# Mixing and decay products as pairs in the two halves of the matmul array, with row differences taken whole from SBUF, in an RWKV block

## The chip, the core and the metric

The kernel runs on one NeuronCore of a Trainium2 chip. The metric is the device time of one execution in microseconds (us); lower is better. The core has five engines with a queue of instructions each: PE (TensorE, matrix products), DVE (VectorE), ACT (ScalarE), POOL (GpSimd) and SP (SyncE, which issues most transfers here). All data are float32. SBUF is the working memory with 128 partitions; products land in PSUM.

## The reference

One RWKV-6 block for 32 sequences of 128 steps and 512 channels, 32 heads of 16. Cut to what matters:

```
xn = layernorm(x, ln1); sx = previous row of xn - xn
xxx = tanh((xn + sx * maa_x) @ maa_w1)            # 5 x 32 columns
x5[m] = xn + sx * (maa_stack[m] + xxx[m] @ maa_w2[m])     # 32 rows of maa_w2 for each m
w = exp(-exp(time_decay + tanh(x5[1] @ decay_w1) @ decay_w2))     # 64 columns, 64 rows
r, k, v = x5[3] @ Wr.T, x5[0] @ Wk.T, x5[2] @ Wv.T;  g = silu(x5[4] @ Wg.T)
for each step:  a = k outer v;  out = r . (u * a + s);  s = a + w * s
x = x + (groupnorm(out) * g) @ Wo.T
xn2 = layernorm(x, ln2); sx2 = previous row of xn2 - xn2
xk = xn2 + sx2 * ffn_maa_k;  xr = xn2 + sx2 * ffn_maa_r
x = x + sigmoid(xr @ Wr'.T) * (square(relu(xk @ Wk'.T)) @ Wv'.T)
```

The `@ maa_w2[m]` (contraction over 32) and `@ decay_w2` (over 64) are the mixing and decay products of the title. The differences to the previous row are taken in both norms.

## The kernel before

The 32 sequences go in 8 groups (`g`) of 4; a group has 512 columns (4 sequences x 128 steps), and the 512 channels stand as 4 blocks (`e`, `f` or `c`) of 128 partitions. Each group passes through these streams, written as Python generators:

- `front_mix`: loads x, normalizes and transposes it (`layernorm_T`), forms the mix `xin`, multiplies by maa_w1 (L414, and L417 with 32 output columns for the fifth mix), tanh, then 20 mixing products (5 mixes x 4 blocks, L435). Each is followed on DVE by two operations that read PSUM (L440 `(p + maa) * sx`, L442 `+ xn`).
- `front_proj`: the decay (L461 with 64 output columns, tanh, 4 products over 64 rows at L469, two exponentials on ACT), then k, r and v with full weights (`matmuls`, L382); `front_gate`: the gate.
- `prep` and the recurrence `rec_*`: 256 units in all. In each, POOL forms k v (L665) and a sum of pairs (L669), ACT copies the decays (L640), DVE scans (L687) and multiplies by r (L689), and PE sums by transposes (L722).
- `back`: group norm, gate, Wo (L810), second norm (`layernorm_T` again), then xk, xr, and the three FFN products (L382, L884, L900). The last group's `back` runs as two halves.

No queue order is left to the hardware. A planner (`Plan`) keeps a list of streams, gives each step a cost and a due time (the table `DUE`), and always emits the step that could start earliest, those within `EPSILON` of it by due time. The order in which it emits is the order of each engine's queue. It also hands out the buffers: "ps" are four PSUM tiles of 128x512 that nearly all products share, "mx" three SBUF tiles, "xnT" and "sx" one each. Steps marked `port=True` are ones that it doesn't plan beside POOL's.

In the before version the small weights are stored so that a mixing product uses the whole array: `w2p` holds for each of four mixes its 32 rows in their own place among zeros, so the contraction runs over all 128 rows of `tha`; the fifth mix shares the tile `dw2m` with the decay.

The row differences and mixes are made block by block in `layernorm_T`'s callback `use`. Each transposed block stays in its PSUM tile. ACT first writes its scaled form to `xnT` (L358), then scales it in place in PSUM (L403, L830); DVE takes the difference or the mix from `xnT` and that PSUM tile (L406 and L408 in the first norm, L833 in the second). For xr ACT writes a scaled copy into a further PSUM tile (L843) and DVE adds (L845).

Of the kernel before, what the change touches and what calls it, by code (L numbers as in the profile page):

```python
# [14 lines left out]
P = 128  # L15
# [23 lines left out]
PE_GAP = 0.04  # L39

# [3 lines left out]
EPSILON = 0.02  # L44


DUE = {"rec": (0.073, 0.928), "mix": (-1.183, -0.487), "proj": (-1.108, 0.725), "gate": (-0.487, 0.788), "prep": (11.173, 11.194), "back": (1.114, 2.212), "last1": (-8.358, -8.236), "last2": (1.752, 11.136)}
# [23 lines left out]
class Plan:  # L71
# [64 lines left out]
    def run(self):  # L136
        while self.streams:
# [32 lines left out]
            for b in op.end:  # L170
                (b if isinstance(b, Buf) else new[b]).open = False
            self.advance(st, new)
# [7 lines left out]
def rwkv6_block(ctx: ExitStack, tc: tile.TileContext, x, prev, s0, vecs, u, maa_w1, maa_w2,  # L180
# [19 lines left out]
    def tag(pool, shape, name, bufs):  # L200
# [13 lines left out]
        (big, [P, N], "tha", 1), (big, [P, N], "th", 2),  # L214
# [9 lines left out]
    ffn = const.tile([P, 3, NE], F32, name="ffn")  # L224
    u_sb = const.tile([P, S], F32, name="u_sb")
    w1_sb = const.tile([P, NE, 5 * XM], F32, name="w1_sb")
    w2p = const.tile([P, 4, E], F32, name="w2p")
    dw1_sb = const.tile([P, NE, XD], F32, name="dw1_sb")

    dw2m = const.tile([P, E], F32, name="dw2m")  # L230
# [8 lines left out]

    nc.gpsimd.memset(thb.t, 0.0)  # L240
    nc.gpsimd.memset(dw2m, 0.0)
    nc.vector.memset(w2p, 0.0)

    def constants():
        nc.sync.dma_start(out=vec, in_=vecs)
        nc.gpsimd.tensor_scalar(ffn[:, 0, :], vec[:, V_FK, :], -1.0, 1.0, ALU.mult, ALU.add)
        nc.gpsimd.tensor_scalar(ffn[:, 2, :], vec[:, V_FR, :], -1.0, 1.0, ALU.mult, ALU.add)
        nc.gpsimd.tensor_tensor(ffn[:, 1, :], ffn[:, 0, :], vec[:, V_LN2B, :], ALU.mult)
        nc.gpsimd.tensor_tensor(ffn[:, 0, :], ffn[:, 0, :], vec[:, V_LN2W, :], ALU.mult)
        nc.sync.dma_start(out=pv, in_=prev)  # L250
        nc.sync.dma_start(out=w1_sb, in_=maa_w1.rearrange("(c p) o -> p c o", p=P))
        for m in range(4):
            nc.sync.dma_start(out=w2p[m * XM : (m + 1) * XM, m, :], in_=maa_w2[m * XM : (m + 1) * XM, :])
        nc.sync.dma_start(out=dw2m[XD : XD + XM, :], in_=maa_w2[4 * XM : 5 * XM, :])
        nc.sync.dma_start(out=dw1_sb, in_=decay_w1.rearrange("(c p) o -> p c o", p=P))
        nc.sync.dma_start(out=dw2m[0:XD, :], in_=decay_w2)
        for e in range(NE):
            nc.sync.dma_start(out=lanes(u_sb, e), in_=u[e * HE : (e + 1) * HE, :].unsqueeze(0).to_broadcast([GB, HE, S]))
# [51 lines left out]
    def layernorm_T(g, src, sums, vw, vb, which, use, take, need=None, bs=range(GB)):  # L310

# [44 lines left out]
        def evict(e, pt):  # L356
            yield Op(ACT, part(0.78, bs), r=[(pt, None)], w=[(xnT, e)])
            nc.scalar.activation(xnT[:, e * GB + b0 : e * GB + b0 + nb_, 1 : L + 1], bt(pt[:, cols]), AF.Identity,  # L358
                                 bias=col(vb, e), scale=col(vw, e))
            yield from use(xnT, e, pt, tiles)  # L360

        for e in range(NE):
            if e == 0:
                pt, *tiles = yield Op(PE, 0.11 * nb_, r=[(xh, None)], w=[(0, None)], alloc=["ps", *take])
            else:
                (pt,) = yield Op(PE, 0.11 * nb_, r=[(xh, None)], w=[(0, None)], alloc=["ps"])
# [7 lines left out]
        return (xnT, *tiles)  # L374

    def row(xnT, e, shift, bs=range(GB)):

        return xnT[:, e * GB + bs[0] : e * GB + bs[-1] + 1, shift : shift + L]

    def matmuls(p, w, xin, e, cols=slice(0, N)):  # L380
        for c in range(NE):
            nc.tensor.matmul(p, lhsT=w[:, c, e * P : (e + 1) * P], rhs=xin[:, c, cols], start=(c == 0), stop=(c == NE - 1))  # L382

# [10 lines left out]
    def front_mix(g, d):  # L394
# [5 lines left out]
        def use(xnT, e, pt, tiles):  # L400

            yield Op(ACT, 0.75, w=[(pt, None)])
            nc.scalar.activation(pt.t, pt.t, AF.Identity, bias=col(V_LN1B, e), scale=col(V_LN1W, e))  # L403
            sx, xin = tiles
            yield Op(DVE, 0.69, r=[(xnT, e), (xnT, "p"), (pt, None)], w=[(sx, e)])
            nc.vector.tensor_tensor(bt(sx[:, e, :]), row(xnT, e, 0), bt(pt.t), ALU.subtract)  # L406
            yield Op(DVE, 0.75, r=[(pt, None), (sx, e)], w=[(xin, e)], end=[pt])
            nc.vector.scalar_tensor_tensor(xin[:, e, :], sx[:, e, :], col(V_MAAX, e), pt.t, ALU.mult, ALU.add)  # L408

        xnT, sx, xin = yield from layernorm_T(g, xt, None, V_LN1W, V_LN1B, 0, use, ("sx", "mx"), need)  # L410
# [5 lines left out]
        for c in range(NE):  # L416
            nc.tensor.matmul(pm2[XD : XD + XM, :], lhsT=w1_sb[:, c, 4 * XM : 5 * XM], rhs=xin[:, c, :],  # L417
                             start=(c == 0), stop=(c == NE - 1))
        (tha,) = yield Op(ACT, 0.6, r=[(pm, None)], w=[(0, None)], alloc=["tha"], end=[pm])
        nc.scalar.activation(tha.t, pm.t, AF.Tanh)  # L420
        yield Op(ACT, 0.6, r=[(pm2, None)], w=[(thb, None)], end=[pm2],
                 need=(lambda: "mixed" in data[g - 1]) if g else None)
        nc.scalar.activation(thb[XD : XD + XM, :], pm2[XD : XD + XM, :], AF.Tanh)

        for m in (1, 0, 3, 2, 4) if g else (1, 0, 2, 3, 4):

            lo, w2 = (tha.t, w2p[:, m, :]) if m < 4 else (thb.t, dw2m)
            x5, late = None, []
            for e in range(NE + 1):
                if e < NE:  # L430
                    if x5 is None:
                        pp, x5 = yield Op(PE, 2 * PASS, r=[(thb, None)], w=[(0, None)], alloc=["ps", "mx"])
                    else:
                        (pp,) = yield Op(PE, 2 * PASS, r=[(thb, None)], w=[(0, None)], alloc=["ps"])
                    nc.tensor.matmul(pp.t, lhsT=w2[:, e * P : (e + 1) * P], rhs=lo, start=True, stop=True)  # L435
                    late.append(pp)
                if e > 0:
                    pp, f = late.pop(0), e - 1
                    yield Op(DVE, 0.75, r=[(sx, None)], w=[(pp, None)])
                    nc.vector.scalar_tensor_tensor(pp.t, pp.t, col(V_MAA + m, f), sx[:, f, :], ALU.add, ALU.mult)  # L440
                    yield Op(DVE, 0.69, r=[(pp, None), (xnT, None)], w=[(x5, f)], end=[pp])
                    nc.vector.tensor_tensor(bt(x5[:, f, :]), bt(pp.t), xnT[:, f * GB : (f + 1) * GB, 1 : L + 1], ALU.add)  # L442
            d["x5", m] = x5
# [3 lines left out]
    def front_proj(g, d):  # L447
# [12 lines left out]
        for c in range(NE):  # L460
            nc.tensor.matmul(pd[0:XD, :], lhsT=dw1_sb[:, c, :], rhs=x5[:, c, :], start=(c == 0), stop=(c == NE - 1))  # L461
        (dlo,) = yield Op(ACT, 0.6, r=[(pd, None)], w=[(0, None)], alloc=["blk"], end=[pd])
        nc.scalar.activation(dlo[0:XD, :], pd[0:XD, :], AF.Tanh)
        late = []
        for e in range(NE + 1):
            if e < NE:
                (p,) = yield Op(PE, 2 * PASS, r=[(dlo, None)], w=[(0, None)], alloc=["ps"],
                                end=[dlo] if e == NE - 1 else [])
                nc.tensor.matmul(p.t, lhsT=dw2m[0:XD, e * P : (e + 1) * P], rhs=dlo[0:XD, :], start=True, stop=True)  # L469
                late.append(p)  # L470
            if e > 0:
                p, f = late.pop(0), e - 1
# [272 lines left out]
    def back(g, d, bs=range(GB), W=None):  # L745
# [81 lines left out]
        def use(xnT, e, pt, tiles):  # L827

            yield Op(ACT, part(0.75, bs), w=[(pt, None)])
            nc.scalar.activation(pt[:, cols], pt[:, cols], AF.Identity, bias=ffn[:, 1, e : e + 1], scale=ffn[:, 0, e : e + 1])  # L830
            (xk,) = tiles
            yield Op(DVE, part(0.75, bs), r=[(xnT, e), (xnT, "p"), (pt, None)], w=[(xk, e)], end=[pt])
            nc.vector.scalar_tensor_tensor(bt(xk[:, e, cols]), row(xnT, e, 0, bs), col(V_FK, e), bt(pt[:, cols]),  # L833
                                           ALU.mult, ALU.add)

        def receptance(xnT):
            xr = None
            for e in range(NE):
                if xr is None:
                    pr, xr = yield Op(ACT, part(0.75, bs), r=[(xnT, e)], w=[(0, None)], alloc=["ps", "mx"])  # L840
                else:
                    (pr,) = yield Op(ACT, part(0.75, bs), r=[(xnT, e)], w=[(0, None)], alloc=["ps"])
                nc.scalar.activation(bt(pr[:, cols]), row(xnT, e, 1, bs), AF.Copy, scale=ffn[:, 2, e : e + 1])  # L843
                yield Op(DVE, part(0.75, bs), r=[(xnT, e), (pr, None)], w=[(xr, e)], end=[pr])
                nc.vector.scalar_tensor_tensor(bt(xr[:, e, cols]), row(xnT, e, 0, bs), col(V_FR, e), bt(pr[:, cols]),  # L845
                                               ALU.mult, ALU.add)
            return xr

# [112 lines left out]
```

## Time and profile before

| | before |
|---|---|
| time, median of 3 runs | 1585.48 us (1584.49 to 1586.62) |
| profiled execution, its own time | 1586.62 us |
| its span, first to last instruction | 1584.8 us |
| PE busy | 1470.4 us |
| DVE busy | 1321.9 us |
| POOL busy | 919.0 us |
| ACT busy | 632.7 us |
| mean granted TensorE clock | 0.974 |

Busy time is the union of an engine's instructions within the span. A float32 product of 128 rows, 128 columns and 512 moving columns appears as two weight loads (PEld) and two matmul instructions, each with its own row; successive ones start 0.429 us apart at full clock, while each lasts some 0.59 us, since they are pipelined. In groups, a row gives line, engine, operation, output<-inputs, shapes and count, then busy time and mean duration, then the idle time just before and what ended it. "The chain" is followed back from the last instruction, at each step to what released it.

### The profile page before, as it was taken

The page shows a single profiled execution, that of the slowest core. Times are in us where ns is not written, and L with a number is a line of the kernel's source. Part 1 is how long each engine was busy: PE and PEld are TensorE (multiplying, and loading weights), DVE is VectorE, ACT ScalarE, POOL GpSimd, SP SyncE. Part 2 cuts the span into 40 slices and gives each one's busy share as a digit, 9 for nine tenths or more (in the row PEclk, how much of TensorE's full clock was granted, in tenths as well). Part 3 has the DMA queues.
Part 4 walks back from the last instruction along what each step waited for, and adds up shares of the span by engine and source line. Part 5 has one row for each costly group of instructions (what it writes and reads, how often), then busy time and mean ns, then how long its engine had stood idle before and what let it go on. Part 6 is the DMA issues. An engine that isn't in the chain of part 4 may idle for free.

```text
span 1584.8 us, 16299 instructions
## 1 busy us (share of the span) xinstructions
PE 1470.4 (93%) x5216; PEld 771.2 (49%) x5216; DVE 1321.9 (83%) x1702; ACT 632.7 (40%) x1213; POOL 919.0 (58%) x549
## 2 busy tenths in 40 slices
PE   5898799899989999999999999999999999978778
PEld 2344354355544554455554555544544555455444
DVE  5539899999989999989979999888988999697642
ACT  4233243345334352444444343443534443336242
POOL 3027683678746694468654694466843884687400
PEclk9999899999999999999999999999999999988989
DMA  6120232514142231423324232332413233240130
GB/s 216 54 83 24 92 97 74 169 60 127 47 143 80 67 120 51 139 88 98 101 71 139 77 117 75 123 104 64 122 50 113 92 107 95 72 140 27 39 121 27
DMA packets 126790, 146.86 MB, mean 93 GB/s; under 512 B 8080, under 2 KB 76304, under 8 KB 125680
## 3 DMA queue, kind: packets, MB, share of 16 engines
q1 hardware_dynamic: 91888, 129.03, 25.0%
q10 hardware_dynamic: 34816, 16.79, 3.7%
q8 instruction: 41, 0.67, 0.2%
q14 instruction: 45, 0.37, 0.1%
HBM read 94.41 MB, written 17.83 MB: 71 GB/s over the span
## 4 chain that ended last, share of the span: by engine, by line
PE 68%; DVE 17%; POOL 8%; issue 3%; ACT 1%; DMA 1%; SPq 0%; DVEq 0%; POOLq 0%
PE ps L382 26%; PE acc L722 10%; PE ps L435 7%; PE ps L884 7%; PE ps L900 6%; PE ps L810 6%; POOL am L665 5%; DVE sc L687 3%; POOL a L669 3%; DVE rm L689 2%; DVE ps L440 2%; PE ps L469 2%; PE ps L461 1%; DVE mx L442 1%; PE ps L417 1%
## 5 line engine op out<-in xcount | busy, mean ns | idle before, releaser
L665 POOL TENSOR_TENSOR am<-v,k 128x1024 f32<-128x1024 f32 x256 | 615.5, 2404 | 211.9 <-DVE k L564 111.2
L382 PE MATMUL ps<-mx,wt 128*128 128x512 f32 (+1 forms) x1312 | 576.3, 587 | 13.4 <-DVE mx L845 5.1
L669 POOL TENSOR_TENSOR a<-am 128x504 f32<-128x504 f32 x256 | 274.9, 1074 | 305.7 <-DVE sc L687 279.0
L382 PEld LDWEIGHTS ps<-mx,wt 128*128 128x128 f32 x1312 | 244.3, 191 | 288.5 <-issue 265.7
L689 DVE TENSOR_TENSOR rm<-sc,r 128x1024 f32<-128x1024 f32 x256 | 312.5, 1221 | 43.1 <-PE acc L722 30.0
L687 DVE TENSOR_TENSOR_SCAN sc<-sc,a 128x512 f32<-128x512 f32 x256 | 312.9, 1222 | 15.9 <-POOL a L669 13.1
L722 PEld LDWEIGHTS acc<-by_head,rm 128*128 128x128 f32 x2176 | 251.6, 143 | 130.9 <-issue 75.1
L722 PE MATMUL acc<-by_head,rm 128*128 128x128 f32 x2176 | 281.4, 276 | 19.7 <-DVE rm L689 12.8
L640 ACT COPY sc<-w 128x512 f32<-128x512 f32 x256 | 151.0, 592 | 233.3 <-DVE rm L689 181.5
L435 PE MATMUL ps<-tha,w2p 128*128 128x512 f32 x256 | 137.2, 634 | 20.7 <-DVE mx L442 5.9
L440 DVE SCALAR_TENSOR_TENSOR ps<-ps,vec,sx 128x512 f32<-128x512 f32 x160 | 119.8, 749 | 39.3 <-PE ps L435 38.9
L651 ACT COPY a<-st 128x8 f32<-128x8 f32 x256 | 50.9, 203 | 189.4 <-DVE sc L687 173.7
L884 PE MATMUL ps<-wt,mx 128*128 128x512 f32 x256 | 115.4, 593 | 4.2 <-DVE mx L408 2.7
L810 PE MATMUL ps<-wt,mx 128*128 128x512 f32 x256 | 116.6, 604 | 1.4 <-DVE x L819 1.4
L442 DVE TENSOR_TENSOR mx<-ps,xnT 128x512 f32<-128x512 f32 x160 | 110.5, 690 | 5.1
L900 PE MATMUL ps<-wt,ev 128*128 128x512 f32 x224 | 100.8, 592 | 0.0
L501 ACT COPY blk<-ps 128x512 f32<-128x512 f32 x96 | 55.9, 583 | 63.1 <-PE ps L382 62.9
L810 PEld LDWEIGHTS ps<-wt,mx 128*128 128x128 f32 x256 | 47.8, 193 | 59.9 <-issue 53.0
L884 PEld LDWEIGHTS ps<-wt,mx 128*128 128x128 f32 x256 | 47.4, 190 | 60.4 <-issue 59.1
L435 PEld LDWEIGHTS ps<-tha,w2p 128*128 128x128 f32 x256 | 43.1, 198 | 61.4 <-issue 21.3
L343 POOL TENSOR_TENSOR rstd<-rstd,mhalf 128x4 f32<-128x4 f32 (+1 forms) x17 | 16.7, 981 | 93.0 <-DVE rstd L341 92.6
L889 DVE SCALAR_TENSOR_TENSOR ps<-th,ps 128x512 f32<-128x512 f32 x32 | 22.1, 689 | 50.6 <-PE ps L900 47.2
(105 smaller groups left out, 1318.0 us busy)
## 6 DMA issues: line engine op xcount, KB each, us to landing
x<-in_x SPq DMA_DIRECT2D x15, 1024.0 KB
wt<-in_wk SPq DMA_DIRECT2D x8, 1024.0 KB
wt<-in_wr SPq DMA_DIRECT2D x8, 1024.0 KB
wt<-in_wg SPq DMA_DIRECT2D x8, 1024.0 KB
dgate<-blk SPq DMA_DIRECT2D x32, 256.0 KB
wt<-in_wo SPq DMA_DIRECT2D x8, 1024.0 KB
wt<-in_fk SPq DMA_DIRECT2D x8, 1024.0 KB
wt<-in_fr SPq DMA_DIRECT2D x8, 1024.0 KB
```

The lines of the kernel that those rows point to most:

```text
L382: nc.tensor.matmul(p, lhsT=w[:, c, e * P : (e + 1) * P], rhs=xin[:, c, cols], start=(c == 0), stop=(c == NE - 1))
L435: nc.tensor.matmul(pp.t, lhsT=w2[:, e * P : (e + 1) * P], rhs=lo, start=True, stop=True)
L440: nc.vector.scalar_tensor_tensor(pp.t, pp.t, col(V_MAA + m, f), sx[:, f, :], ALU.add, ALU.mult)
L640: nc.scalar.copy(sc.t, d["w01"][:, q : q + 1, :].to_broadcast([P, DH, T2]))
L665: nc.gpsimd.tensor_tensor(am.t, v[:, ds, :], k[:, q : q + 1, :].to_broadcast([P, DH, L]), ALU.mult)
L669: nc.gpsimd.tensor_tensor(a[:, :, 1:T2], am2[:, :, 0 : T2 - 1, 0], am2[:, :, 0 : T2 - 1, 1], ALU.add)
L687: nc.vector.tensor_tensor_scan(scf, scf, a.t.rearrange("p d n -> p (d n)"), 0.0, ALU.mult, ALU.add)
L689: nc.vector.tensor_tensor(pair(rm.t), sc.t.unsqueeze(3).to_broadcast([P, DH, T2, 2]), r2[:, q : q + 1, :, :].to_broadcast([P, DH, T2, 2]), ...
L722: nc.tensor.matmul(acc[:, i, :], lhsT=rm[:, i, :], rhs=by_head, is_transpose=True, start=(q == 0 and i % 4 == 0), stop=(q == S), skip_grou ...
L810: nc.tensor.matmul(p.t, lhsT=att[:, c, b * L : (b + 1) * L], rhs=wot[:, c, :], start=(c == 0), stop=(c == NE - 1))
L884: nc.tensor.matmul(p.t, lhsT=xr[:, c, b * L : (b + 1) * L], rhs=frt[:, c, :], start=(c == 0), stop=(c == NE - 1))
L900: nc.tensor.matmul(p2.t, lhsT=kv[:, c, b * L : (b + 1) * L], rhs=fvt[:, c, :], start=(c == 0), stop=(c == NE - 1))
```

## The change

- A mixing product contracts over 64 rows (32 of weights, 32 of zeros), a decay product over its 64. Two products, of two neighbouring column blocks of the output, are issued one after the other (`side_by_side`): one in the upper half of the array's rows, one in the lower half, into two PSUM tiles. The small weights (`w2p`, `dw2p`) hold the even blocks in partitions 0 to 63 and the odd blocks in 64 to 127.
- The low-rank rows must stand in both halves: `tha` gets a second plane with its halves exchanged (two more tanh of 64 partitions each), the fifth mix's columns of maa_w1 stand twice in `w1_sb` (so that L417's product has 96 output columns), and decay_w1 stands twice (128 output columns).
- The two evictions of each product are streams of their own (`mixed`), due right after the pair; a pair waits in the plan until all but one of the earlier products are evicted.
- The constants come in 26 loads in place of 14.
- The row differences and mixes change too: ACT only writes `xnT`, DVE takes one difference over the whole tile (`sx`), and `mix` makes xin, xk and xr by one operation per block, with both inputs in SBUF. The in-place scalings on ACT, the callback `use`, `receptance` and the tile `ffn` go.
- The planner's price for a pair is `PAIR`; the due times and `EPSILON` have other values.

```
+PAIR = 2.6 * PASS
-EPSILON = 0.02
+EPSILON = 0.0284
-DUE = {"rec": (0.073, 0.928), "mix": (-1.183, -0.487), "proj": (-1.108, 0.725), "gate": (-0.487, 0.788), "prep": (11.173, 11.194), "back": (1.114, 2.212), "last1": (-8.358, -8.236), "last2": (1.752, 11.136)}
+DUE = {"rec": (-0.719, 0.83), "mix": (-2.052, -0.463), "proj": (-0.981, -0.21), "gate": (-0.039, 0.771), "prep": (-0.013, 0.421), "back": (1.215, 2.03), "last1": (-10.118, 2.886), "last2": (-4.571, -2.72)}
...
+        for i, m in ((0, 1), (1, 2), (2, 0), (3, 3), (4, 4), (6, 4)):
+            nc.sync.dma_start(out=w1_sb[:, :, i * XM : (i + 1) * XM], in_=w1v[:, :, m * XM : (m + 1) * XM])
+        for h in range(2):
+            for m in range(5):
+                r = h * XD + (XM if m in (2, 3) else 0)
+                nc.sync.dma_start(out=w2p[r : r + XM, m, :].rearrange("r (f p) -> r f p", p=P),
+                                  in_=halves(maa_w2[m * XM : (m + 1) * XM, :], h))
...
+        (sx,) = yield Op(DVE, part(2.3, bs), r=[(xnT, None)], w=[(0, None)], alloc=["sx"], port=True)
+            nc.vector.tensor_tensor(
+                sx.t.rearrange("p e (b t) -> p (e b) t", t=L), xnT[:, :, 0:L], xnT[:, :, 1 : L + 1], ALU.subtract)
...
+    def mix(xnT, sx, v, bs=range(GB)):
+        for e in range(NE):
...
+            nc.vector.scalar_tensor_tensor(bt(o[:, e, b0 * L : b1 * L]), bt(sx[:, e, b0 * L : b1 * L]), col(v, e),
+                                           xnT[:, e * GB + b0 : e * GB + b1, 1 : L + 1], ALU.mult, ALU.add)
...
+    def side_by_side(pp, w, up, low):
+        for p, h, t in zip(pp, (slice(0, XD), slice(XD, P)), (up, low)):
+            nc.tensor.matmul(p.t, lhsT=w[h, :], rhs=t[h, :], start=True, stop=True)
...
+        nc.scalar.activation(tha[:, 0, :], pm.t, AF.Tanh)
+        nc.scalar.activation(tha[0:XD, 1, :], pm[XD:P, :], AF.Tanh)
+        nc.scalar.activation(tha[XD:P, 1, :], pm[0:XD, :], AF.Tanh)
...
+            for i in range(2):
+                pp = yield Op(PE, PAIR, r=[(thb, None), (tha, None)], w=[(0, None), (1, None)],
+                              alloc=["ps", "ps"] + ([] if i else ["mx"]), need=lambda: done[1] >= done[0] - 1)
+                side_by_side(pp, w2p[:, m, i * P : (i + 1) * P], up, low)
+                done[0] += 2
+                plan.add(mixed(m, i, pp, x5), plan.due, plan.due + 0.02, 4)
...
+        for i in range(2):
+            pp = yield Op(PE, PAIR, r=[(dlo, None)], w=[(0, None), (1, None)], alloc=["ps", "ps"], end=[dlo] if i else [])
+            side_by_side(pp, dw2p[:, i * P : (i + 1) * P], dlo.t, dlo.t)
```

## The prediction

> **What bounds the kernel now.** I read the page first (busy shares, then the chain that ended last), then the busy time by stretch, then the groups by line, and last the TensorE timeline around the products that the change moves.
>
> ```profile
> PE 1470.4 (93%) x5216; PEld 771.2 (49%) x5216; DVE 1321.9 (83%) x1702; ACT 632.7 (40%) x1213; POOL 919.0 (58%) x549
> ...
> PE 68%; DVE 17%; POOL 8%; issue 3%; ACT 1%; DMA 1%; SPq 0%; DVEq 0%; POOLq 0%
> ```
>
> ```profile
> 500.00:700.00 200.00, 193.27 (x712) 102.06 (x711) 181.51 (x228) 84.64 (x165) 130.17 (x76) 1.00 0.32 102
> 700.00:900.00 200.00, 195.77 (x715) 103.36 (x714) 180.36 (x228) 86.76 (x168) 129.74 (x77) 1.00 0.30 93
> ```
>
> The columns of the second view are stretch, length, then busy time of PE, PEld, DVE, ACT and POOL. In the steady middle PE is busy for 97 to 98% and DVE for 90%. So PE sets the pace, its chain share says the same, and DVE is only some 7% behind: a saving on PE counts until DVE is reached. ACT, with 42%, sets nothing.
>
> ```profile
> L435 PE MATMUL ps<-tha,w2p 128*128 128x512 f32 x256 | 137.2, 634 | 20.7 <-DVE mx L442 5.9 <-DVE a L615 5.7 <-ACT thb L423 4.4
> L435 PE MATMUL ps<-thb,dw2m 128*128 128x512 f32 x64 | 32.2, 595 | 1.6 <-DVE mx L442 1.6
> L469 PE MATMUL ps<-blk,dw2m 64*128 64x512 f32 x64 | 35.6, 652 | 5.6 <-DVE mx L442 2.6 <-DVE mx L801 2.2 <-DVE x L819 0.8
> L403 ACT ACTIVATE ps<-ps,vec 128x512 f32<-128x512 f32 x32 | 24.0, 750 | 0.9
> L406 DVE TENSOR_TENSOR sx<-xnT,ps 128x512 f32<-128x512 f32 x32 | 21.8, 680 | 21.7 <-ACT ps L403 21.6
> L408 DVE SCALAR_TENSOR_TENSOR mx<-sx,vec,ps 128x512 f32<-128x512 f32 x32 | 23.9, 748 | 1.1
> L833 DVE SCALAR_TENSOR_TENSOR mx<-xnT,vec,ps 128x512 f32<-128x512 f32 (+1 forms) x36 | 24.4, 678 | 17.9 <-ACT ps L830 17.9
> L845 DVE SCALAR_TENSOR_TENSOR mx<-xnT,vec,ps 128x512 f32<-128x512 f32 (+1 forms) x36 | 23.9, 678 | 1.1 <-ACT ps L843 0.8
> ```
>
> The first three rows are the 160 mixing and 32 decay products: each is two matmul instructions (320 and 64). The other rows are the row differences and mixes that the change rebuilds.
>
> ```profile
> 1225.27 1.98 PE L469 MATMUL ps<-blk,dw2m 64*128 64x512 f32 x4
> 1227.18 1.09 PE L722 MATMUL acc<-by_head,rm 128*128 128x128 f32 x8
> 1228.20 1.12 PE L469 MATMUL ps<-blk,dw2m 64*128 64x512 f32 x2
> 1229.26 1.09 PE L722 MATMUL acc<-by_head,rm 128*128 128x128 f32 x8
> 1230.19 1.02 PE L435 MATMUL ps<-tha,w2p 128*128 128x512 f32 x2
> 1231.05 3.60 PE L810 MATMUL ps<-wt,mx 128*128 128x512 f32 x8
> ```
>
> Starts (first column) tell what a product costs. A full-array one takes 0.86 us (1230.19 to 1231.05), two passes of 0.429. A 64-row one between full-array work takes 1.06 (1228.20 to 1229.26). From the single starts of all 25 visits of L469 to the 64-row mode: the step into it is 523 ns in place of 429, the first step inside 533, the step out 519; a visit costs 94 + 104 + 90 = 0.29 us.
>
> **The change, part by part.**
>
> *PE before.* 192 products x 0.858 = 164.7 us; 25 visits x 0.288 = 7.2; the products of 32 and 64 output columns (L417, L461) are also left and entered at 522 ns, 16 x 0.186 = 3.0. Sum 174.9 us. *PE after.* In the built program the 96 pairs stand in 81 visits, 72 of one pair alone, and the narrow forms are gone: 81 x 0.288 = 23.3 us, plus the passes. How far two products in the two halves overlap, no row shows. Best: fully, 2 passes a pair, 96 x 0.858 = 82.4, sum 105.7, so 69 us less. Worst: not at all, 4 passes, 164.7 + 23.3 = 188.0, so 13 us more. Between them: each product is two instructions, and the second product's first instruction can run beside the first product's second at the earliest if instructions start strictly in order; then a lone pair takes 3 passes, a run of k pairs 2k+1, in all 273 x 0.429 = 117.1 + 23.3 = 140.4, 34.5 us less. I take overlap, midway between 2 and 3 passes: 52 us less, and keep 2, 3 and 4 for the range.
>
> The Trainium skill weighs in here ("TensorE: Matmul & The Clock Gate", Part 3): matmuls start and end strictly in program order, and four 32-row tiles gained 3.07 times, each a single instruction. By its ordering rule the pair costs three passes and the time would be the upper end of my forecast; no run here shows it yet.
>
> *DVE.* Removed: 21.8 + 23.9 + 24.4 + 23.9 = 94.0 us. Added: one difference over the whole normalized tile, 15 whole and 2 half; the nearest row of that size is L779 (128x2048), 2.293 whole and 1.226 half: 36.8 us. And 88 whole mixes at 0.748 (L408) and 16 half ones at 0.480 (halves of L845): 73.5 us. Sum 110.3, so 16 us more. The mixing evictions (L440, L442) stay as many.
>
> *The port.* The removed operations read PSUM on one side. The added ones have both inputs in SBUF, as POOL's have, and such rows are stretched while POOL runs:
>
> ```profile
> L585 DVE TENSOR_TENSOR w<-w 128x1008 f32<-128x1008 f32 x8 | 20.6, 2572 | 0.0
> L696 DVE TENSOR_TENSOR rm<-v,rk 128x1024 f32<-128x1024 f32 x16 | 27.0, 1690 | 2.0 <-PE acc L722 1.9
> L699 DVE TENSOR_TENSOR ps<-v,a 128x512 f32<-128x512 f32 x16 | 18.3, 1145 | 0.1
> ```
>
> Alone they take 1.19, 1.22 and 0.69 us (their instances with POOL idle); L406 and L408 don't change beside POOL. All 111 larger operations of this kind in the trace lost 39 us, 0.35 each. The change adds 121, of which some 108 stand beside the recurrence: 108 x 0.35 = 38 us. Bounds: none (POOL waits for DVE for 279 us, so gaps exist) and 108 x 1.38 (L585) = 149. I take 38, since L696 and L699, which stand inside the recurrence as the new ones do, lost 0.47 and 0.45, and others at a group's edge nothing. DVE then has 1321.9 + 16 + 38 = 1376 us.
>
> *ACT.* L403, L830 and L843 go (24.0 + 25.3 + 22.6), two more tanh per group come (16 x 0.59): 62 us less. ACT carries 1% of the chain, so nothing directly. The 40 us for which DVE stood waiting for ACT at L406 and L833 go too; what is late next there is the eviction L358, for which the whole difference must wait four times over. The further tanh delay the first pair by 1.2 us; recurrence products stand ahead of it on PE.
>
> *PSUM.* A pair takes two of the four "ps" buffers at once, and PE, which is in order, holds all matmuls behind a pair that waits for DVE to free the second. Against that, the tiles of the norms are freed after one operation instead of three or four. Nothing net; by the idle time ahead of L435 (22 us) it is worth from -22 to +22.
>
> *Start and end.* 26 loads of constants for 14 push the weight loads back on SP: 12 x 0.45 us = 5 us. By the timeline they are issued from 10.6 us on, and by the chain the first is multiplied at 57.4: hidden; without that cover, +5. In three norms (the first, and the two halves at the end) nothing else runs: the difference and four mixes come after the last eviction instead of one of each, ACT's share leaves; about 1 us each, 3 in all.
>
> *Order.* All due times differ, so every engine's order is new. PE idles 3% in the middle; I give this nothing, within 10 us either way.
>
> **The sum.** PE's saving passes on by its share of the chain, 0.68, since the rest is set by others; DVE's gain in work by 0.17. From the span 1584.8: -52 x 0.68 = -35; +54 x 0.17 = +9; +3; span 1562. Profiled time stood 1.8 above its span, and the median 1.1 below the profiled time of 1586.6: about **1563 us**. With 3 passes -23.5 in place of -35: 1574; with 2 passes -47: 1551. Forecast case: 1548 to 1577.
>
> **Rivals.**
>
> *DVE takes the bound, slower.* With DVE at 1376 us, and 263 us of idle today of which only the 40 us on ACT vanish, the time is 1376 + 223 = 1599. For it: DVE is at 90% in the middle, and each stretched operation sits ahead of scan and product of the recurrence. Against: 136 us of DVE's idle time are waits for PE (L689, L440, L889, L819), which shrink when PE is freed. It decides from a stretch of 0.22 us an operation if none of those waits shrink (16 + 108 x 0.22 = 40), later if they do; 1585 to 1612.
>
> *The halves don't overlap, slower.* PE has 13 us more, passed on at 0.68: +9, +9 and +3 as above: 1584.8 + 21, plus 0.7, 1607. This is also the way in which the change doesn't do what it says. For it: no row of the trace shows two matmuls at once. Against: the two use different rows and different banks.
>
> *The gain comes through whole.* The pairs take 2 passes, DVE's stretch finds gaps, and PE's saving is passed on at 0.85 (DVE's share of the chain, which is largely waiting for PE, goes with it): 1584.8 - 59 + 16 x 0.17 + 3 = 1532. Against: DVE, with 1338 us of work and 130 us of idle before 100 and after 1400 us, would have to be all but free of waits between.
>
> **How the numbers follow.** Forecast case 0.60; DVE bound 0.18; no overlap 0.12; below 1548 0.06; a cancelling of gain and loss 0.04. A measurement of this kernel can tell about 0.2% (3 us) from no change. Faster: 0.60 + 0.06 = 0.66, to which a mild DVE bound adds nothing; same 0.05 (the cancelling, and 0.01 of the DVE case's lower edge); slower 0.17 + 0.12 = 0.29. The range runs from 1538 to 1606: it takes in the forecast case, most of the DVE case and part of the rest.
>
> **What would show it.** In the changed profile: starts of the two products of a lone pair to the next full-array matmul, about 1.15 us (two passes), 1.58 (three) or 2.0 (none); PE's busy time near 1420; DVE's near 1376 with the new difference at 2.3 to 3.5 us and the mixes at 0.75 to 1.2; ACT near 571. The prediction is wrong in its main step if the pair takes 4 passes, and in its price of DVE if the mixes average over 1.3 us or if PE falls below 90% in the middle with no shorter time.

## The result, and the profile after

The changed kernel takes 1634.12 us (median of 4 runs, 1631.22 to 1636.82) against 1586.05 us for the kernel before on the same chip: 1.0304 times as long, 95% interval 1.0284 to 1.0324. The profiled execution took 1636.82 us, its span 1635.0. Forecast was 1563 us; the time lies 28 us above the upper end of the range.

First the page, in the order in which before was read:

```profile
PE 1450.0 (89%) x5216; PEld 760.7 (47%) x5216; DVE 1352.0 (83%) x1687; ACT 572.7 (35%) x1125; POOL 917.4 (56%) x545
...
PEclk8789899889999999999999999999999999997979
...
PE 45%; DVE 32%; POOL 10%; issue 5%; DMA 4%; ACT 2%; SPq 1%; ACTq 1%; DVEq 0%; POOLq 0%
```

PE's busy time fell by 20 us, and its share of the chain from 68 to 45%. DVE's work rose by 30 us. The clock that PE was granted, one digit for a slice of 41 us, is lower at many places of the first third: 0.948 in the mean, against 0.974. In the clock's own records PE stood at half clock for 171 us of the span, against 82 before; 96 us of the 171 lie ahead of 472 us.

The middle by stretches (length, then busy PE, PEld, DVE, ACT, POOL), each from one group's first recurrence unit to the next one's:

```profile
664.00:855.00 191.00, 178.17 (x650) 92.56 (x649) 170.96 (x208) 70.70 (x139) 114.39 (x67) 0.97 0.29 95
855.00:1042.00 187.00, 174.06 (x647) 90.33 (x646) 169.80 (x207) 69.45 (x139) 113.30 (x66) 0.99 0.30 97
1042.00:1230.00 188.00, 175.01 (x650) 90.86 (x649) 170.77 (x208) 70.45 (x139) 114.18 (x67) 0.99 0.30 96
```

The same three groups before (633 to 1181 us), summed, with the means of one:

```profile
sum 548.00, PE 532.35 PEld 279.56 DVE 493.82 ACT 233.12 POOL 340.68; mean PE 177.45 PEld 93.19 DVE 164.61 ACT 77.71 POOL 113.56
```

A group takes 188.7 us, against 182.7 before. DVE is busy for 170.5 of it (164.6 before), PE for 175.8 (177.5): PE is no longer near 100%, and DVE isn't either. The first unit starts at 136.9 us instead of 124.0; the last one lies 52 us later than before.

So 13 of the 52 us are lost before the recurrence begins. The chain runs there, in both kernels, through the second load of x, for which DVE's statistics wait. First before, then after (the wait of L323 or L326: us in total, times, longest; the load: start, length):

```profile
DVE stats L323 <- DMA x<-in_x: 6.8, 2, 3.5
14.70 10.93 DMA x<-in_x
```

```profile
DVE stats L326 <- DMA x<-in_x: 14.4, 2, 10.5
22.59 10.84 DMA x<-in_x
```

SyncE issues that load 7.9 us later, and the first weight load at 18.56 us instead of 10.60, because the 12 more loads of constants stand ahead of both in its queue.

The products and the rebuilt mixes, by groups:

```profile
L403 PE MATMUL ps<-tha,w2p 64*128 64x512 f32 x256 | 86.3, 667 | 18.4 <-DVE mx L450 18.2
L403 PE MATMUL ps<-thb,w2p 64*128 64x512 f32 x64 | 21.2, 657 | 3.2 <-DVE mx L450 3.2
L403 PE MATMUL ps<-blk,dw2p 64*128 64x512 f32 x64 | 20.6, 647 | 1.3 <-DVE mx L450 1.1
...
L392 DVE SCALAR_TENSOR_TENSOR mx<-sx,vec,xnT 128x512 f32<-128x512 f32 (+1 forms) x104 | 83.3, 862 | 3.8 <-PE ps L398 2.9
L375 DVE TENSOR_TENSOR sx<-xnT 128x2048 f32<-128x2048 f32 x15 | 34.8, 2317 | 19.0 <-ACT xnT L361 19.0
```

The 192 products' busy time fell from 205.0 to 128.1 us. Two lone pairs on TensorE's timeline (start, length):

```profile
783.28 1.13 PE L403 MATMUL ps<-thb,w2p 64*128 64x512 f32 x4
784.34 1.09 PE L741 MATMUL acc<-by_head,rm 128*128 128x128 f32 x8
785.27 3.60 PE L398 MATMUL ps<-mx,wt 128*128 128x512 f32 x8
788.80 1.13 PE L403 MATMUL ps<-thb,w2p 64*128 64x512 f32 x4
789.86 1.09 PE L741 MATMUL acc<-by_head,rm 128*128 128x128 f32 x8
```

Four matmul instructions, two products, take 1.06 us until the next full-array one: as much as one lone 64-row product before. In the single starts they come in twos, 6 to 7 ns apart, the second two 527 ns later. So the halves overlap fully.

Some 55 us earlier in the same group a pair does less well:

```profile
725.78 1.12 PE L403 MATMUL ps<-tha,w2p 64*128 64x512 f32 x2
728.48 1.12 PE L403 MATMUL ps<-tha,w2p 64*128 64x512 f32 x2 [1.58 <-DVE mx L450]
729.53 1.19 PE L741 MATMUL acc<-by_head,rm 128*128 128x128 f32 x8
731.05 8.49 PE L829 MATMUL ps<-wt,mx 128*128 128x512 f32 x16 [0.33 <-DVE x L838]
```

The pair is torn apart: its second product waits 1.58 us, PE being in order, until DVE has emptied a PSUM tile (L450). PE was granted half clock from 730.4 us for 3.4 us, after 3.4 us in which it had been busy for about half of the time (1.9 us); the 16 instructions of L829 take 8.3 us up to the next start, against 6.9 at full clock.

### The profile page after: what moved, and what is told of

Same layout as the page of the kernel before. It is cut to its first block, busy times and chain, and to the rows that moved or that the text cites. A ratio compares the mean times of both kernels' runs of the same rounds, so it can differ in the third digit from the quotient of the medians.

```text
span 1635.0 us, 16245 instructions
## 1 busy us (share of the span) xinstructions
PE 1450.0 (89%) x5216; PEld 760.7 (47%) x5216; DVE 1352.0 (83%) x1687; ACT 572.7 (35%) x1125; POOL 917.4 (56%) x545
## 4 chain that ended last, share of the span: by engine, by line
PE 45%; DVE 32%; POOL 10%; issue 5%; DMA 4%; ACT 2%; SPq 1%; ACTq 1%; DVEq 0%; POOLq 0%
PE ps L398 19%; POOL am L684 6%; PE acc L741 6%; DVE sc L706 6%; PE ps L829 5%; PE ps L898 4%; PE ps L882 4%; DVE rm L708 4%; PE ps L403 4%; POOL a L688 3%; DVE ps L448 3%; DVE mx L450 2%; DMA v<-blk 2%; DVE mx L392 2%; PE ps L484 2%
## 5 line engine op out<-in xcount | busy, mean ns | idle before, releaser
L398 PE MATMUL ps<-mx,wt 128*128 128x512 f32 (+1 forms) x1312 | 592.4, 601 | 24.8 <-DMA wt<-in_wk 10.4
L688 POOL TENSOR_TENSOR a<-am 128x504 f32<-128x504 f32 x256 | 280.2, 1095 | 438.9 <-DVE sc L706 404.7
L398 PEld LDWEIGHTS ps<-mx,wt 128*128 128x128 f32 x1312 | 249.5, 198 | 302.5 <-issue 271.4
L741 PE MATMUL acc<-by_head,rm 128*128 128x128 f32 x2176 | 287.7, 281 | 50.9 <-DVE rm L708 34.0
L829 PE MATMUL ps<-wt,mx 128*128 128x512 f32 x256 | 118.7, 612 | 5.7 <-DVE x L838 5.4
L450 DVE TENSOR_TENSOR mx<-ps,xnT 128x512 f32<-128x512 f32 x160 | 110.4, 690 | 4.9
L403 PE MATMUL ps<-tha,w2p 64*128 64x512 f32 x256 | 86.3, 667 | 18.4 <-DVE mx L450 18.2
L392 DVE SCALAR_TENSOR_TENSOR mx<-sx,vec,xnT 128x512 f32<-128x512 f32 (+1 forms) x104 | 83.3, 862 | 3.8 <-PE ps L398 2.9
L829 PEld LDWEIGHTS ps<-wt,mx 128*128 128x128 f32 x256 | 48.3, 196 | 64.6 <-issue 52.2
L361 ACT ACTIVATE xnT<-ps,vec 128x512 f32<-128x512 f32 (+1 forms) x68 | 49.0, 749 | 38.3 <-PE ps L367 36.4
```

The costliest lines, as they stand in the source:

```text
L403: nc.tensor.matmul(p.t, lhsT=w[h, :], rhs=t[h, :], start=True, stop=True)
L688: nc.gpsimd.tensor_tensor(a[:, :, 1:T2], am2[:, :, 0 : T2 - 1, 0], am2[:, :, 0 : T2 - 1, 1], ALU.add)
L741: nc.tensor.matmul(acc[:, i, :], lhsT=rm[:, i, :], rhs=by_head, is_transpose=True, start=(q == 0 and i % 4 == 0), stop=(q == S), skip_grou ...
L829: nc.tensor.matmul(p.t, lhsT=att[:, c, b * L : (b + 1) * L], rhs=wot[:, c, :], start=(c == 0), stop=(c == NE - 1))
```

## The experiments

Three theories of the loss: the freed time on PE is worth less than its chain share says (DVE and PE hold each other, and the clock falls in the gaps); it is the work that the SBUF mixes add on DVE; or it is the order that the due times make.

**Parts of the change, with the due times as they are.** Four kernels mix the two forms of the row differences ("blocks" as before, "whole" as changed), single products or pairs, and the two sets of due times with their `EPSILON`. The edits are whole parts of the diff shown above; for `pairs_blocks_olddue`:

```
 the kernel before
+ side_by_side, mixed, the loads of w1_sb, w2p, dw1_sb, dw2p, PAIR
  (layernorm_T with use, receptance, ffn, DUE, EPSILON as before)
```

> The changed kernel with the row differences and mixes of the kernel before (block by block, from PSUM, with ACT's in-place scalings); pairs, due times and EPSILON as changed. If the loss sits in the whole differences and SBUF mixes (more DVE work, shared port), it goes: 1585 or less. If it sits in the due times or in the pairs, it stays: 1615 to 1645.

Measured: 1725.49 us (1.0877, 1.0848 to 1.0905).

> The pairs alone: everything else, due times and EPSILON too, as in the kernel before. If the pairs are worth what TensorE saves on them (69 us of its work, passed on at 0.68), 1540 to 1555. If the pairs themselves cost more than they save (bunched evictions, TensorE idling and its clock falling), 1600 to 1640. If due times or mixes carry the whole loss, about 1540 to 1570.

Measured: 1697.13 us (1.0696, 1.0677 to 1.0715).

> The whole differences and SBUF mixes with the due times and EPSILON of the changed kernel, but the products single and padded as before. If pairs save time where they are, this is slower than the changed kernel by up to 47 us: 1650 to 1680. If the pairs are what costs, it is faster than 1634: 1590 to 1620.

Measured: 1726.14 us (1.0885, 1.0860 to 1.0910).

> The changed kernel with due times and EPSILON of the kernel before. If the order that follows from the new due times is the loss, 1550 to 1590. If not, 1620 to 1660.

Measured: 1715.57 us (1.0811, 1.0791 to 1.0831).

All four lie above everything that was expected. One kernel, the changed one, takes 1634 or 1716 us by seventeen numbers that change no work, only its place. The planner says so itself: its own end for these four is 1749, 1728, 1698 and 1728 us, against 1582 for the kernel before and 1585 for the changed one. So these due times don't serve another form of the kernel, and the parts can't be priced under another's numbers: none of these four tells what a part costs.

**TensorE's time at a fixed order.** Every instruction keeps its place in its queue; only its duration changes.

```
 same_half, from the changed kernel:
-        for p, h, t in zip(pp, (slice(0, XD), slice(XD, P)), (up, low)):
+        for p, h, t in zip(pp, (slice(0, XD), slice(0, XD)), (up, low)):
 before_bf16_mix, from the kernel before; the tile "tha" is bfloat16:
-            lo, w2 = (tha.t, w2p[:, m, :]) if m < 4 else (thb.t, dw2m)
+            lo, w2 = (tha.t, w2p[:, m, :].bitcast(BF16)[:, 1::2]) if m < 4 else (thb.t, dw2m)
```

> The changed kernel with every instruction in its place, but both products of a pair in the upper half of the array, so that they can't overlap (the odd blocks are computed from the even blocks' rows). TensorE has 96 x 0.86 = 82 us more work at the same order. If TensorE's time still sets the end of the changed kernel, 1690 to 1715. If the overlap frees time that nothing uses (other engines or the order set the end, and the clock falls in the gaps), 1634 to 1660.

Measured: 1658.22 us (1.0445 of before, 1.0414 to 1.0477): 24 us over the changed kernel for 82 us of work. The overlap is worth 24 us where it is: a factor of 0.29, at the upper edge of the range for "time that nothing uses".

> The kernel before with the same order, but 128 of its 160 mixing products in bfloat16 (tha written as bfloat16, the weights' upper halves read as bfloat16), one pass each: 128 x (0.858 - 0.215) = 82 us less work for TensorE, and nothing else moved. If a saving on TensorE passes on at its share of the chain, 1530. If at this order other engines and a falling clock eat it, 1560 to 1586.

Measured: 1581.11 us against 1585.64 (0.9968, 0.9957 to 0.9980): 4.5 us for 82, a factor of 0.055; this lies in the range named for "other engines and a falling clock eat it". From its page:

```profile
PE 1414.3 (90%) x5070; PEld 746.5 (47%) x5088; DVE 1324.1 (84%) x1702; ACT 633.5 (40%) x1213; POOL 920.7 (58%) x549
...
PEclk9899799899999999999999999999999999988989
```

PE's busy time fell by 56 of the 82 us. Much of the rest came back through the clock: 140 us at half clock instead of 82, with nothing changed but the 128 matmuls in bfloat16. PE was busy at half clock for 95 us instead of 51, and half of the difference is 22 us. DVE is as busy as before, and the span hardly moved.

**DVE's time at a fixed order, and both.**

```
-nc.vector.scalar_tensor_tensor(pp.t, pp.t, col(V_MAA + m, f), sx[:, f, :], ALU.add, ALU.mult)
+nc.vector.scalar_tensor_tensor(pp[:, 0 : N // 2], pp[:, 0 : N // 2], col(V_MAA + m, f), sx[:, f, 0 : N // 2], ALU.add, ALU.mult)
```

> The kernel before with the same order, but the first eviction of each mixing product (L440, 160 of them) over half its columns, so that half of each mix is left out: from 0.749 to about 0.48 us each, 43 us less work for DVE and nothing else moved. If DVE's chain is what sets the pace (82 us off TensorE gave 4.5), 1545 to 1565. If neither engine alone sets it and the order's handovers do, 1578 to 1586.

Measured: 1572.51 us against 1586.99 (0.9910, 0.9889 to 0.9930). DVE's busy time fell by 37 us; 14.5 us came through, a factor of 0.39. The time lies between the two ranges: neither expectation was met.

> Both at once, at the same order: 128 mixing products in bfloat16 and the first eviction over half its columns (half of each mix left out): 82 us off TensorE and 43 us off DVE. If DVE alone sets the pace, as the last one or a few us less. If the two engines hold each other, so that only work taken from both counts, clearly less than the sum of the two alone: 1510 to 1545.

Measured: 1550.63 us (0.9762, 0.9747 to 0.9777). 36 us, where the two alone sum to 19; for engines that hold each other 1510 to 1545 had been expected, so the direction was met and the size was not. The pages of the two kernels, first `before_dve_half`, then `before_both`:

```profile
PE 1463.4 (93%) x5216; PEld 771.3 (49%) x5216; DVE 1284.5 (82%) x1702; ACT 632.4 (40%) x1213; POOL 920.0 (59%) x549
```

```profile
PE 1401.6 (90%) x5074; PEld 743.4 (48%) x5088; DVE 1282.6 (83%) x1702; ACT 632.7 (41%) x1213; POOL 919.9 (59%) x549
```

With DVE's work cut as well, the same cut on PE brings 22 us (1572.51 to 1550.63) instead of 4.5. The two engines hold each other: what one gains is worth more once the other has gained too.

> The changed kernel at its own order, with the first eviction of each mixing product (L448) over half its columns, so that half of each mix is left out: 43 us less work for DVE, as taken from the kernel before, where it gave 14.5. If DVE's added work is what the changed kernel loses by, more comes through here, where TensorE is freed already: 1595 to 1612. If it loses by its order and the clock instead, as much as before or less: 1618 to 1630.

Measured: 1619.81 us (1.0215 of before, 1.0195 to 1.0235): 14.3 us less than the changed kernel, with 39 us less busy time on DVE, a factor of 0.36 as before. It lies in the range named for a loss by the order and the clock. By this factor the 30 us that DVE does more in the changed kernel are worth about 11 us, an estimate.

**Due times of their own.** To price the parts fairly, the due times were searched anew for the two mixed forms, by the planner's own end. The kernel before and the changed one keep their own.

```
 pairs_blocks_retuned_b: pairs alone, blocks as before, and
+EPSILON = 0.0918
+DUE = {"rec": (0.083, 1.173), "mix": (-1.765, -0.783), "proj": (-1.417, 1.064), "gate": (-0.452, 0.914), "prep": (3.181, 12.436), "back": (0.974, 2.69), "last1": (-11.233, -15.446), "last2": (6.641, 15.72)}
```

> The pairs alone, everything else as in the kernel before, but with due times searched anew for this kernel with the kernel's own planner (a search of its due times and EPSILON; the planner's end is then 4 us ahead of what it gives the kernel before). If the order is what decides and the pairs cost nothing themselves, 1570 to 1605. If the pairs themselves cost (bunched evictions, gaps in which the clock falls), 1615 to 1650.

Measured: 1616.25 us (1.0178, 1.0163 to 1.0193).

> The same from another start of the search, to see how far two orders that the planner holds equal lie apart on the chip. Within 10 us of the first if the planner's prices hold on the chip; 20 to 40 apart if the chip's lag behind the plan depends on the order.

Measured: 1598.72 us (1.0069, 1.0052 to 1.0086): 18 us from the first, though the planner has them 1.5 us apart: more than the 10 expected if the planner's prices held, and less than the 20 to 40 of the other case.

> The pairs alone with a third set of due times, found by a longer search (the planner's end is 8.6 us ahead of the kernel before). If the planner's gain came through, 1577; if the chip lags behind plans with pairs by 20 to 40 us, as in the two others, 1593 to 1613.

Measured: 1611.17 us (1.0154, 1.0137 to 1.0171): best for the planner of the three, and not on the chip.

> The whole differences and SBUF mixes alone, products single and padded as before, due times searched anew for it (the planner's end is 38 us behind that of the kernel before). If the mixes from SBUF are the structural loss, 1620 to 1665, slower than or equal to the changed kernel; if they cost nothing by themselves, 1590 to 1610.

Measured: 1640.44 us (1.0327, 1.0310 to 1.0344).

| | blocks, from PSUM | whole, from SBUF |
|---|---|---|
| single products | 1586 (before) | 1640 |
| pairs | 1599, 1611, 1616 | 1634 (changed) |

Each cell has due times of its own, and those differ by up to 18 us within a cell, so the table is rough. Within that, the whole differences are the costly half of the change, by 18 to 54 us. The pairs lose 13 to 30 us in one column and win 6 in the other.

**Where the chip falls behind the plan.** The planner's own start of every instruction was set beside the trace, in the same order. The lag is how much later than planned a DVE scan (one in each unit of the recurrence) starts on the chip, in us; below zero it starts earlier:

| | plan ends | chip, median | lag of the first and last scan |
|---|---|---|---|
| before | 1582 | 1586 | 4, 10 |
| pairs alone, a, b, c | 1577, 1579, 1573 | 1616, 1599, 1611 | 13, 35; 12, 18; 14, 42 |
| whole differences alone | 1619 | 1640 | -6, 19 |
| changed | 1585 | 1634 | 13, 50 |

The plan of the changed kernel ends only 3 us behind that of the kernel before (1584.9 and 1581.8): nearly all of its loss is lag. What the whole differences cost when they stand alone is in their plan already, 38 us; what the pairs lose is not.

The first scan of every kernel with pairs comes late: at 132 to 142 us, against 113 to 126 in those with single products. In all with pairs the second load of x is issued at 22.6 to 22.9 us, in the others at 14.2 to 15.0. The planner has no price for the loads of constants. So the 12 more loads very likely make some 8 of the 13 us at the start, though no run changed them alone.

Later, from 472 to 1227 us, the changed kernel's lag grows from 12 to 46 us. In the same groups PE stood at half clock for 27 us, against 7 before; at half speed that costs at most some 10 us more. In the group from 664 to 855 us the lag grows by 10 us, in a few jumps of DVE that are partly made up again: about 2.4 us at L790, a 128x128 operation on SBUF stretched while POOL runs,

```profile
688.30 0.40 DVE L789 TENSOR_SCALAR th<-th 128x128 f32<-128x128 f32 x1
688.74 2.39 DVE L790 TENSOR_SCALAR th<-th 128x128 int32<-128x128 int32 x1
691.16 0.23 DVE L791 TENSOR_SCALAR th<-th 128x128 int32<-128x128 int32 x1
```

some 5 us from 724 to 737 us, around the torn pair shown above (up to 1.6 of them by its wait, up to 1.4 by the half clock), and about 2 us at each of L715, the norm's transposes and one stretched mix.

## Why the prediction was wrong, point by point

- *The sum, "PE's saving passes on by its share of the chain, 0.68"*: this is the first step that failed. At fixed orders the factor is 0.055 in the kernel before and 0.29 in the changed one. A PE that is busy for 97% and holds 68% of the chain was not a bound that could be moved alone.
- *"Order: I give this nothing, within 10 us"*: this is the second, and it turned the sign. With the measured factors the sum would read -20 for PE (69 x 0.29), +11 for DVE (30 x 0.36) and +3: some 6 us faster, an estimate. The kernel is 48 us slower, so some 54 us stand in no priced term. They show as lag behind the plan: 50 us at the last scan, against 10 before, of which 13 stand at the first. How much an order can be worth on the chip is shown by two plans that end 1.5 us apart and run 18 us apart.
- *"Start and end", the loads "hidden"*: wrong too. The 12 more loads took SyncE 8 us, not 5, and the chain passes through a load behind them; the first unit starts 13 us later.
- *What a pair costs*: the mechanism was right, the size better than the 52 us taken. A lone pair takes 1.06 us plus 0.09 for the step in, 1.15 as given for two passes, so PE lost 69 us of work; the visit's 94, 104 and 90 ns held. By the ordering rule of the Trainium skill ("TensorE: Matmul & The Clock Gate", Part 3) it would have been three passes; the starts 7 ns apart differ, and the measurement decides.
- *The clock*, not in the sum at all. PE ran busy at half clock for 119 us instead of 51; half of the difference, 34 us, is work done twice as slowly, and half of the 69 us saved. `before_bf16_mix` shows that shorter matmuls lengthen the time at half clock at an unchanged order. But 68 of the 119 us lie ahead of 472 us, where the lag doesn't grow. The Trainium skill (the same page, Part 1) says that the clock is throttled by default and released by activity, judged in windows of some 3.4 us; the stretches at half clock here are multiples of 3.4 us.
- *DVE*: its busy time was put at 1376 us and came to 1352. The added work was right (16 us and some), the stretch too large: the mixes lost 16 us and the whole difference none, not 38 in all; 12 of the 88 whole mixes were stretched, to 1.4 or 2.8 us, the others took some 0.745. But a microsecond on DVE was worth 0.36 to 0.39 us, not 0.17.
- *ACT* (571 put, 572.7 found): right; what its time is worth was not measured.
- *The rival "DVE takes the bound"* named the right side, with a time 35 us too low. Its mechanism is a part: in the middle the period grew by 6.0 us a group and DVE's work by 5.9, which looks like a bound, yet taking 39 us off DVE returned 14.
- *Open*: the cause of the lag that grows between 472 and 1227 us. Half clock (at most some 10 us of it), torn pairs and stretched operations are seen in it, but how it splits between them and the order was not separated. Whether the start's 13 us would come back with fewer loads was not tested.

## What to carry to other kernels

Before a saving on the busiest engine is counted, shorten its work at a fixed order (a cheaper data type, fewer columns) and see what comes through: here 82 us gave 4.5, while the same cut together with 37 us off the second engine gave 36. In a kernel whose order is planned offline, a change of durations is a change of order, which can be worth more than the change itself. Ask the planner first: here its plan ended 3 us later, not 22 earlier. Compare two forms only with orders made for each, and measure several orders that the planner holds equal. Count the loads that are put ahead of the first data. And where the clock falls when an engine idles, as here, part of what is saved is given back.

## What the runs showed of the hardware that was not expected

Two float32 products in the two row halves start their passes 6 to 7 ns apart and take 1.06 us together between full-array work, although each is two instructions on the same rows. And the granted TensorE clock can fall when work is taken away: 82 us less matmul time at an unchanged order raised the time at half clock from 82 to 140 us.
